# Feed-forward rows sorted by expert and gathered in tiles of 128, weights addressed by a register, output projection of two blocks moved up

## The chip, the cores and the metric

The kernel runs on one core of one Trainium2 chip. The metric is the device time of one execution in microseconds (us), the median of several runs. TensorE is called PE, VectorE DVE, ScalarE ACT, GpSimd POOL and SyncE SP, as in the profile. SP computes nothing here; it issues DMAs.

## The reference

One transformer layer on 2048 rows of 256 numbers (fp32). Attention has 16 heads of 128; its four weight matrices are stored as codes times scales for blocks of 32 input rows. The feed-forward part is a mixture of 8 experts with an inner size of 176. A router scores the experts, the two best are kept, and their outputs are summed with weights.

```python
def attn(x):   # q, k, v, out: w = codes * repeat(scales, 32)
    scores = einsum('bqhd,bkhd->bhqk', q, k) / sqrt(128)
    return mxfp4_matmul(softmax(scores) @ v, wo) + bo
def ffn(x):
    probs = softmax(x @ Wr)                    # 8 experts
    topk_w, topk_idx = top_k(probs, 2); topk_w /= topk_w.sum(-1)
    combine = sum over k of topk_w * one_hot(topk_idx, 8)
    h = silu(x @ Wg[e]) * (x @ Wu[e])          # every expert, 256 -> 176
    return sum over e of combine[:, e] * (h @ Wd[e])
x = x + layernorm(attn(layernorm(x)))
x = x + layernorm(ffn(layernorm(x)))
```

The reference computes all eight experts for every row; six of the eight have the weight zero in each row.

## The kernel before, in words

Everything is written out by hand in one program: a manual schedule, in which the order of the Python calls is the order of the instructions on each engine. The rows form 4 blocks (`b`) of 512, each of 4 tiles of 128.

The attention loop (`for g in range(NS + 2)`, 256 steps of one head and one tile of 128 query rows) takes some 1590 of the 1877 us. Each step makes scores in two halves (L453 to L457), a row maximum on DVE (L458), exponentials on ACT (L469), and a high and a low fp16 part of the probabilities (L483 on ACT, L498 on DVE), which two DMA transposes on SP's queue (L486, L502) turn into `pt`. The product with v (`pv_unit`, `pv_part`, L517 to L519) follows 13 half-steps behind (`PVLAG`). A finished head and block is cast on POOL (L531, L532) into `o`, a high and a low fp16 part, and stored by POOL's queue to `ot_d` in DRAM (L533). In the last head, `late(t)` also loads and dequantizes `wo`, loads the gate weights `wg` in four pieces (`load_gu`, L612) and splits each into a rounded part and a remainder in fp32r[...] (`split_gu`, `split_piece`: ACT L603, POOL L605), and begins to load block 0's `oi` (`load_oi`, L632), the attention output in pieces of four heads and 256 rows, on SP's queue.

After the last scores, `pv_unit(UEND)` to `pv_unit(UEND + 8)` finish the last block. Between them lie, for block 0, the output projection (`op_pass`, `op_mm`, L759: 64 products of 256 columns for half a block), the residual and both norms (`ln_a` to `ln_c`), the transposes of the normed rows (`tr`, L821) and the router (`router_a` to `router_d`). The router keeps the two best experts and writes a table of weights, 8 experts by 512 rows, to DRAM (`ct_d`, L886). The output projection of block 1 follows, then the loop.

The feed-forward loop (`for q in range(4 * NCH + 2)`) runs over 4 blocks and 11 chunks of 128 of the 8 x 176 = 1408 inner columns of all experts. `gate_up(b, c)` makes 12 products of 512 columns (L914: gate and up, two halves of the input, three products of high and low parts each), then a sigmoid (ACT L934), three multiplications on DVE (L935, L936, L939), one with `cu`, the routing weight spread over the chunk's rows by `load_cu` (L897), and a split into a rounded part (ACT L927) and a remainder (POOL L928). `down(b, c)`, two chunks later, adds 12 products of 256 columns (L953) to a block's sum. Output projection, norms and routers of blocks 2 and 3 are hooked into the chunks of earlier blocks (`FIRST`, `PREP`, `PREP2`); `fin1`, `fin2` (L786) and `fin_last` norm the sum and add it.

PE, ACT, DVE, POOL and SP each work through their own queue in order; a tile pool with few buffers makes a writer wait for the last reader. `psS` and `psA` are the pools of PSUM, where products are summed.

Of the kernel before, what the change touches and what calls it, by code (L numbers as in the profile page):

```python
# [33 lines left out]
POOL_COLS = 512  # L34
# [3 lines left out]
def sandwich(  # L38
# [28 lines left out]
    ct_d = [dram.tile([E, 512], F32, name=f"ct_d{b}") for b in range(4)]  # L67
# [9 lines left out]
    def rstd_of(mv, n, pool):  # L77
        v = pool.tile([128, n], F32, name="ln_v")
        nc.vector.tensor_scalar(v, mv[:, :, 1], EPS, None, ALU.add)
        r = pool.tile([128, n], F32, name="ln_r")  # L80
        nc.gpsimd.tensor_tensor(r, v, nhalf[:, :n], ALU.pow)
        return r
# [9 lines left out]
    rw = const.tile([128, 2, 2, E], F32R)  # L92
    res = const.tile([128, 2, NH], F32)

    def tail_consts(i):
# [5 lines left out]
        else:  # L101
# [6 lines left out]
            nc.gpsimd.tensor_tensor(rw[:, 1], rst, rw[:, 0].bitcast(F32), ALU.subtract)  # L108

# [48 lines left out]
    psS = ctx.enter_context(tc.tile_pool(name="psS", bufs=3, space=PSUM))  # L158
# [443 lines left out]
    def split_piece(dst, stg, on_pool):  # L602
        nc.scalar.copy(dst[0], stg)  # L603
        eng = nc.gpsimd if on_pool else nc.vector
        eng.tensor_tensor(dst[1], stg, dst[0].bitcast(F32), ALU.subtract)  # L605

    gu_raw = {}

    def load_gu(src, i, pool, tag, bufs, eng=None):
        kc, eh = divmod(i, 2)  # L610
        stg = pool.tile([128, 4, I], F32, name="gu_raw", tag=tag, bufs=bufs)
        (eng or nc.sync).dma_start(  # L612
            out=stg,
            in_=src.rearrange("e (kc p) i -> kc p e i", p=128)[kc][:, 4 * eh : 4 * eh + 4],
        )
        return stg

    def split_gu(dst, i, stg, on_pool):
        kc, eh = divmod(i, 2)
        cs = slice(4 * I * eh, 4 * I * eh + 4 * I)  # L620
        split_piece(
            (dst[:, 0, kc, cs], dst[:, 1, kc, cs]),
            stg.rearrange("p e i -> p (e i)"), on_pool,
        )

    OIN = {}

    def load_oi(b, half, j, tag="kT"):
        oi = kqv.tile(
            [128, 4, 2, 256], HP, name="oi", tag=tag, bufs={"kT": 8, "v": 7}[tag]  # L630
        )
        nc.sync.dma_start(  # L632
            out=oi, in_=ot_d[b][:, 4 * j : 4 * j + 4, :, bass.ts(half, 256)]
        )
        OIN[(b, half, j)] = oi

# [4 lines left out]
    gw = None  # L641
# [3 lines left out]
    WG_LOAD = (7, 9, 10, 11)  # L645

    def late(t):
        nonlocal gw
        if t in WO_LOAD:
            load_wo(3 + WO_LOAD.index(t), kqv, ("kT", "kT"), 8)  # L650
        if t - 1 in WO_LOAD:
            dequant_wo(3 + WO_LOAD.index(t - 1))
        if t == 13:
            bias_row2(gst.pop("b3"))
        if t == 12:
            gst["b3"] = bias_row()
        if t == 9:
            proj_ctx.close()
            rp = ctx.enter_context(tc.tile_pool(name="gw", bufs=1, side="right"))
            gw = rp.tile([128, 2, 2, EI], F32R)  # L660
        if 10 <= t < 14:
            split_gu(gw, t - 10, gst.pop(t - 10), True)
        if t in WG_LOAD:
            i = WG_LOAD.index(t)
            gst[i] = load_gu(wg, i, kqv, "kT", 8)
        if t == 9:
            load_oi(0, 1, 0, "v")
        if 11 <= t < 15:
            load_oi(0, 0, t - 11)

    X1 = {}
    XV = x.rearrange("b (c t p) d -> p (b c) t d", p=128, t=4)

    defer = False
    prev2 = None
    for g in range(NS + 2):
# [10 lines left out]
        if g == NS:  # L687
            load_oi(0, 1, 1)
            load_oi(0, 1, 2)
            load_oi(0, 1, 3)  # L690
# [41 lines left out]
        if g == NS:  # L732
            X1[0] = kqv.tile([128, 4, D], F32, name="x1_0", tag="kT", bufs=8)
            nc.sync.dma_start(out=X1[0], in_=XV[:, 0])
    UEND = 2 * (NS + 2)


    AT, MV, XT, CT = {}, {}, {}, {}

    OPS = {}  # L740

    def aux_psum(shape, dtype, name, tag):
        if tag == "s":
            return psS.tile(shape, dtype, name=name + "_s", tag="s", bufs=3)
        return psA.tile(shape, dtype, name=name, tag=tag)

    def op_mm(b, half, js, tag="pj"):
        if js[0] == 0:
            if half == 0:
                AT[b] = uwp.tile([128, 4, D], F32, name="at", bufs=2)  # L750
                MV[b] = small.tile([128, 4, 2], F32, name="mv")
            OPS[(b, half)] = aux_psum([128, 2, D], F32, "op", tag)
        ps = OPS[(b, half)]
        for j in js:
            oi = OIN.pop((b, half, j))
            for t in range(2):
                for hh in range(4):
                    for hl in range(2):
                        nc.tensor.matmul(  # L759
                            ps[:, t], oi[:, hh, hl, bass.ts(t, 128)],  # L760
                            wo[j // 2][:, 4 * (j % 2) + hh, :],
                            start=(j == 0 and t == 0 and hh == 0 and hl == 0),
                            stop=(j == 3 and t == 1 and hh == 3 and hl == 1),
                        )
        if js[-1] == 3:
            at = AT[b]
            tt = slice(2 * half, 2 * half + 2)
            nc.vector.scalar_tensor_tensor(
                at[:, tt], ps, sig[:, 0, 2:3],
                crow.unsqueeze(1).to_broadcast([128, 2, D]), ALU.mult, ALU.add,  # L770
            )
            stats(at, MV[b], 2 * half, 2 * half + 2)

    def op_pass(b, half, tag="pj"):
        op_mm(b, half, (0, 1, 2, 3), tag)

    def stats(src, mv, t0, t1):
        bs = small.tile([128, 4, 6], F32, name="bs")
        for t in range(t0, t1):
            nc.vector.bn_stats(bs[:, t], src[:, t, :])  # L780
        for t in range(t0, t1):
            nc.vector.bn_aggr(mv[:, t, :], bs[:, t])

    def norm(dst, src, mv, r):
        for t in range(4):
            nc.vector.tensor_scalar(  # L786
                dst[:, t, :], src[:, t, :], mv[:, t, 0:1], r[:, t : t + 1],
                ALU.subtract, ALU.mult,
            )

    R1, R2, MV2 = {}, {}, {}

    def ln_a(b):
        R1[b] = rstd_of(MV[b], 4, small)

    def ln_b1(b):
        norm(AT[b], AT[b], MV[b], R1[b])
        nc.vector.tensor_tensor(X1[b], AT[b], X1[b], ALU.add)

    def ln_b2(b):  # L800
        MV2[b] = small.tile([128, 4, 2], F32, name="mv2")
        stats(X1[b], MV2[b], 0, 4)
        R2[b] = rstd_of(MV2[b], 4, small)

    def ln_c(b):
        norm(AT[b], X1[b], MV2[b], R2[b])

    def tr(b, kc, tag="pj"):
        xn = AT[b]
        if kc == 0 and b == 0:  # L810
            XT[b] = [
                kqv.tile([128, 2, 512], F32R, name="xT0", tag="v", bufs=7)
                for _ in range(2)
            ]
        elif kc == 0:
            xt = tl.tile([128, 2, 2, 512], F32R, name="xT", bufs=2)
            XT[b] = [xt[:, 0], xt[:, 1]]
        xh, xl = XT[b]
        ps = aux_psum([128, 512], F32, "trp", tag)
        for t in range(4):  # L820
            nc.tensor.transpose(ps[:, bass.ts(t, 128)], xn[:, t, bass.ts(kc, 128)], ident)  # L821
        nc.scalar.copy(xh[:, kc], ps)
        nc.vector.tensor_tensor(xl[:, kc], ps, xh[:, kc].bitcast(F32), ALU.subtract)

    LGT, LG, CW = {}, {}, {}

    def router_a(b, tag="pj"):
        xT = XT[b]
        ps = aux_psum([8, 512], F32, "rp", tag)
        n = 0  # L830
        for kc in range(2):
            for a, w in ((0, 0), (1, 0), (0, 1)):
                nc.tensor.matmul(
                    ps, rw[:, w, kc, :], xT[a][:, kc, :], start=(n == 0), stop=(n == 5)
                )
                n += 1
        if b == 0:
            LGT[b] = kqv.tile([8, 512], F32, name="lgT0", tag="v", bufs=7)
        else:
            LGT[b] = tl.tile([8, 512], F32, name="lgT", tag="sg", bufs=3)  # L840
        nc.scalar.copy(LGT[b], ps)

    def router_b(b, tag="pj"):
        ps = aux_psum([128, 4, 8], F32, "lgp", tag)
        for t in range(4):
            nc.tensor.transpose(ps[:, t], LGT[b][:, bass.ts(t, 128)], ident[:8, :8])
        lg = small.tile([128, 4, 8], F32, name="lg", bufs=1)
        nc.vector.tensor_copy(lg, ps)
        mx = small.tile([128, 4, 8], F32, name="mx", bufs=1)
        ix = small.tile([128, 4, 8], U32, name="ix", bufs=1)  # L850
        for t in range(4):
            nc.vector.max(mx[:, t, :], lg[:, t, :])
# [166 lines left out]
    for j in range(4):  # L1019
        load_oi(1, 0, j)  # L1020
# [154 lines left out]
```

## Time and profile before

| | us |
|---|---|
| median of 3 runs | 1890.71 |
| lowest, highest | 1884.35, 1891.69 |
| profiled execution, its own time | 1879.05 |
| its span, first to last instruction | 1877.3 |
| last scores end at about | 1582 |
| first and last product of the feed-forward loop | 1640.7, 1870 |
| granted TensorE clock, mean | 0.99 |

The profile shows one execution. Each engine's busy time counts neither waiting nor sequencer work. Times in the stage table and the timelines count from the span's start. "Idle before, releaser" says how long an engine stood still ahead of an instruction, and what ended the wait. In the chain of waits each step is followed back to what released it.

### The profile page before, as it was taken

How to read it: one execution, taken by the hardware profiler on the slowest of the kernel's cores; microseconds unless marked ns; L12 is line 12 of the kernel's file. 1: busy time of each engine (PE TensorE's matmuls, PEld its weight loads, DVE VectorE, ACT ScalarE, POOL GpSimd, SP SyncE). 2: the span in 40 equal slices, each digit the busy share in tenths (PEclk: the TensorE clock that was granted, in tenths of full speed). 3: DMA queues.
4: the chain of work that ended last, by engine and by line, in shares of the span. 5: the costliest groups of instructions: out<-in, count | busy, mean ns of one | idle time of the engine just before them, and what ended most of it. 6: DMA issues, size and time to landing. Idle time of an engine off the chain costs nothing. (4 is left out here: it accounts for less than half of the span.)

```text
span 1877.3 us, 25533 instructions
## 1 busy us (share of the span) xinstructions
PE 1794.1 (96%) x8890; PEld 936.0 (50%) x8890; DVE 1632.4 (87%) x2267; ACT 1365.5 (73%) x1730; POOL 907.5 (48%) x893
## 2 busy tenths in 40 slices
PE   7899999999999999999999999999999988899998
PEld 4344444444444444444444444444444434588887
DVE  7999989998999899998999999889999886458566
ACT  5888878888888788887888888778888776123232
POOL 3554574457544654465445644564444342233222
PEclk9999999999999999999999999999999999999999
DMA  3999999999999999999999999999999999982121
GB/s 91 190 193 190 189 202 198 190 189 202 196 191 189 193 195 191 192 201 193 188 190 205 197 189 192 183 202 194 191 186 205 208 220 219 259 236 69 55 71 57
DMA packets 1133345, 342.31 MB, mean 182 GB/s; under 512 B 1070896, under 2 KB 1120768, under 8 KB 1133216
## 3 DMA queue, kind: packets, MB, share of 16 engines
q1 hardware_dynamic: 1120528, 310.53, 90.4%
q0 software_dynamic: 9584, 27.82, 5.9%
q10 hardware_dynamic: 3104, 2.33, 0.5%
q8 instruction: 70, 1.15, 0.2%
q14 instruction: 59, 0.48, 0.1%
HBM read 53.22 MB, written 18.94 MB: 38 GB/s over the span
## 5 line engine op out<-in xcount | busy, mean ns | idle before, releaser
L498 DVE SCALAR_TENSOR_TENSOR pl<-p,m,ph 128x1024 f16<-128x1024 f32 x512 | 731.6, 1429 | 50.2 <-DMA pt<-pl 43.9
L469 ACT ACTIVATE p<-s,m,ssc 128x1024 f32<-128x1024 f32 x512 | 611.9, 1199 | 192.6 <-DVE m L462 158.9
L458 DVE TENSOR_REDUCE m<-s 128x1 f32<-128x1024 f32 x512 | 622.0, 1215 | 23.2 <-PE s L457 22.7
L483 ACT ACTIVATE ph<-p,m 128x2048 f16<-128x2048 f32 x256 | 513.0, 2004 | 84.7 <-issue 30.2
L518 PE MATMUL pv<-pt,v 128*128 128x512 f16 x1024 | 391.2, 382 | 27.9 <-DMA pt<-pl 27.9
L453 PE MATMUL s<-kT,qT 128*128 128x512 f16 x1024 | 389.9, 381 | 16.9 <-ACT p L469 13.9
L517 PE MATMUL pv<-pt,v 128*128 128x512 f16 x1024 | 390.6, 381 | 7.4 <-DMA pt<-ph 5.3
L519 PE MATMUL pv<-pt,v 128*128 128x512 f16 x1024 | 391.2, 382 | 0.0
L454 PE MATMUL s<-kT,qT 128*128 128x512 f16 x1024 | 389.8, 381 | 0.0
L457 PE MATMUL s<-kT,qT 128*128 128x512 f16 x1024 | 305.3, 380 | 0.0
L205 POOL CAST qT<-t 128x512 f16<-128x512 f32 x63 | 86.4, 1371 | 247.2 <-ACT t L204 247.2
L236 POOL CAST v<-t 128x256 f16<-128x256 f32 (+1 forms) x105 | 54.3, 517 | 271.8 <-ACT t L235 271.8
L518 PEld LDWEIGHTS <-v 128*128 128x128 f16 x1024 | 100.7, 98 | 153.8 <-issue 29.4
L454 PEld LDWEIGHTS <-qT 128*128 128x128 f16 x1024 | 100.4, 98 | 135.2 <-issue 33.4
L517 PEld LDWEIGHTS <-v 128*128 128x128 f16 x1024 | 100.6, 98 | 130.8 <-issue 7.0
L519 PEld LDWEIGHTS <-v 128*128 128x128 f16 x1024 | 100.7, 98 | 123.6 <-issue 7.6
L457 PEld LDWEIGHTS <-qT 128*128 128x128 f16 x1024 | 100.5, 98 | 121.8 <-issue 1.7
L453 PEld LDWEIGHTS <-qT 128*128 128x128 f16 x1024 | 100.6, 98 | 111.3 <-issue 3.2
L237 POOL TENSOR_TENSOR v<-t,v 128x256 f16<-128x256 f32 (+1 forms) x105 | 146.8, 1398 | 8.4
L928 POOL TENSOR_TENSOR hh<-sg,hh 128x512 fp32r<-128x512 f32 x42 | 54.5, 1298 | 144.6 <-ACT hh L927 99.4
L927 ACT CAST hh<-sg 128x512 fp32r<-128x512 f32 (+1 forms) x45 | 27.5, 611 | 118.4 <-DVE sg L939 118.4
L206 POOL TENSOR_TENSOR kT<-t,kT 128x512 f16<-128x512 f32 x60 | 107.8, 1796 | 5.0
(184 smaller groups left out, 2019.4 us busy)
## 6 DMA issues: line engine op xcount, KB each, us to landing
oi<-ot_d SPq DMA_DIRECT2D x32, 512.0 KB, 6.9
ot_d<-o POOLq DMA_DIRECT2D x63, 256.0 KB, 4.1
pt<-ph SPq DMA_TRANSPOSE x256, 5.1
pt<-pl SPq DMA_TRANSPOSE x256, 4.7
cu<-ct_d SPq DMA_DIRECT2D x16, 256.0 KB, 3.9
xt<-in_L_attn_x SPq DMA_DIRECT2D x4, 512.0 KB, 5.6
wos<-in_L_attn_wo_scales ACTq DMA_DIRECT2D x32, 64.0 KB, 4.5
woc<-in_L_attn_wo_codes SPq DMA_DIRECT2D x8, 256.0 KB, 3.5
```

What stands on the lines that cost most here:

```text
L206: nc.gpsimd.tensor_tensor(t[:, 1, :], t32, t[:, 0, :], ALU.subtract)
L237: nc.gpsimd.tensor_tensor(v[:, 1, sl, :], t32, v[:, 0, sl, :], ALU.subtract)
L453: nc.tensor.matmul(s[:, j, :], q[:, 0, qc], k[:, 0, :], start=True, stop=False)
L454: nc.tensor.matmul(s[:, j, :], q[:, 0, qc], k[:, 1, :], start=False, stop=False)
L457: nc.tensor.matmul(s[:, j, :], q[:, 1, qc], k[:, 0, :], start=False, stop=True)
L458: nc.vector.tensor_reduce(m[:, half : half + 1], s, AX.XY, ALU.max)
L469: nc.scalar.activation(p[:, bass.ts(i, 1024)], s, AF.Exp, bias=m[:, 2:3], scale=ssc[:, 0:1], accum_out=m[:, 3 + i : 4 + i],)
L483: nc.scalar.activation(ph, p, AF.Copy, scale=m[:, 6:7])
L498: nc.vector.scalar_tensor_tensor(pl[:, cs], p[:, cs], m[:, 6:7], ph[:, cs], ALU.mult, ALU.subtract)
L517: nc.tensor.matmul(ps, vh, d[:, :, c, :], start=(c == 0), stop=False)
L518: nc.tensor.matmul(ps, vh, d[:, :, 16 + c, :], start=False, stop=False)
L519: nc.tensor.matmul(ps, vl, d[:, :, c, :], start=False, stop=(c == 15))
```

## The change

The feed-forward part is rebuilt for the chosen experts alone.

- **Sorting.** Two groups of 1024 rows (two blocks) are sorted apart. `router_c` makes one-hot rows of the two chosen experts. `places(G)` counts, by products with a triangle and with ones, how many rows of each expert lie ahead of a row, rounds each expert's count up to a multiple of 128, and so gives each of the 2048 row-expert pairs a place (`POS`) among 23 tiles of 128. `slot_rows(G)` inverts this: which row lies in which place (`ROWS`). `TE[G]` holds for each tile the expert's offset in the weights. 23 tiles hold any routing.
- **Rows.** `rows16(b)` writes each normed row (times 64) as a high and a low fp16 part to DRAM (`xr_d`). `load_xg(q)` gathers 128 rows by an indirect DMA on POOL's queue, `turn_xg(q)` turns them by a DMA transpose on SP's queue.
- **Tiles.** 46 tiles in place of 44 chunks. `ff_up(q)` loads the tile's offset from SBUF into a register of PE and makes 6 products of 352 columns (gate and up of one expert side by side), addressed by the register; then a sigmoid on ACT and two DVE operations. `ff_tr(q - 1)` turns the result by two fp32 transposes, and `ff_down(q - 2)` makes 6 products of 256 columns, addressed too; the sum is copied by ACT and stored by SP to `ys_d`. In the program each of the 552 addressed products has an instruction of register arithmetic ahead of it on PE.
- **Result.** `gather(b, u)` fetches both results of a row by indirect DMAs on POOL (four per 256 rows), `combine` weights, sums and takes statistics, `finish_rows` norms, adds and stores. The routing weight is applied here.
- **Weights** become fp16 high and low parts instead of fp32r ones, scaled by powers of two that are found at run time (`largest`, `scale_gu_a` to `_c`, `squares`, `scale_d_a`, `_b`); they are loaded and split after the attention (`load_raw`, `split_raw`).
- **Moves.** The output projection of blocks 2 and 3 goes from the loop to the stage ahead of it; that of block 1 goes ahead of `pv_unit(UEND + 1)`. Block 0's eight `oi` loads go from SP's queue to POOL's. Two of four norms go from DVE to ACT (`normed`). `load_cu`, `ct_d`, `fin*` and the splits of the last head are gone.

The diff, cut to its core:

```diff
     def load_oi(b, half, j, tag="kT", eng=None):
...
-        nc.sync.dma_start(
+        (eng or nc.gpsimd).dma_start(
             out=oi, in_=ot_d[b][:, 4 * j : 4 * j + 4, :, bass.ts(half, 256)]
...
     def late(t):
...
-        if 10 <= t < 14:
-            split_gu(gw, t - 10, gst.pop(t - 10), True)
-        if t in WG_LOAD:
-            i = WG_LOAD.index(t)
-            gst[i] = load_gu(wg, i, kqv, "kT", 8)
-        if t == 9:
-            load_oi(0, 1, 0, "v")
-        if 11 <= t < 15:
-            load_oi(0, 0, t - 11)
+        if t == 11:
+            loads(0, 0, (0, 1, 2), "g")
+        if t == 13:
+            loads(0, 0, (3,), "g")
+            loads(0, 1)
...
+    def slot_rows(G, tag="pj"):
+        lo, hi = SL.pop(G)
+        ps = aux_psum([128, GT], F32, "slp", tag)
+        for i in range(16):
+            nc.tensor.matmul(ps, lo[:, i], hi[:, i], start=(i == 0), stop=(i == 15))
+        ROWS[G] = P["ff"].tile([128, GT], I32, name="rows", bufs=2)
+        nc.vector.tensor_copy(ROWS[G], ps)
...
+    def load_xg(q):
+        G, j = divmod(q, GT)
+        xr = P["ff"].tile([128, 512], HP, name="xq", bufs=5)
+        nc.gpsimd.indirect_dma_start(
+            out=xr, out_offset=None, in_=xr_d[G],
+            in_offset=bass.IndirectOffsetOnAxis(ap=ROWS[G][:, j : j + 1], axis=0),
+        )
+        XQ[q] = xr
+
+    def turn_xg(q):
+        XG[q] = P["ff"].tile([128, 4, 128], HP, name="xg", bufs=4)
+        nc.sync.dma_start_transpose(out=XG[q], in_=XQ.pop(q))
+
+    def ff_up(q):
+        G, j = divmod(q, GT)
+        REG[q] = nc.values_load(
+            TE[G][0:1, j : j + 1], engines=(mybir.EngineType.PE,), min_val=0,
...
+        ps = P["psF"].tile([128, 2 * I], F32, name="gup", bufs=2)
+        n = 0
+        for kc in range(2):
+            for a, w in ((0, 0), (0, 1), (1, 0)):
+                nc.tensor.matmul(
+                    ps, xg[:, 2 * a + kc, :], GU[(w, kc)].rearrange("p e n -> p (e n)")[
+                        :, bass.ds(REG[q], 2 * I)
+                    ],
+                    start=(n == 0), stop=(n == 5),
+                )
+                n += 1
+        sg = P["ff"].tile([128, I], F32, name="sg", bufs=2)
+        nc.scalar.activation(sg, ps[:, :I], AF.Sigmoid, scale=sgs)
+        h = P["ff"].tile([128, I], F32, name="h", bufs=2)
+        nc.vector.tensor_tensor(sg, sg, ps[:, :I], ALU.mult)
+        nc.vector.scalar_tensor_tensor(h, sg, HC, ps[:, I : 2 * I], ALU.mult, ALU.mult)
...
+    def ff_tr(q):
...
+        for c in range(2):
+            nc.tensor.transpose(ps[:, c], h[:, bass.ts(c, IC)], ident)
+        hh = P["ff"].tile([IC, 2, 2, 128], HP, name="hh", bufs=2)
+        nc.scalar.copy(hh[:, 0], ps)
+        nc.vector.tensor_tensor(hh[:, 1], ps, hh[:, 0], ALU.subtract)
...
+    def ff_down(q):
...
+                nc.tensor.matmul(
+                    ps, hh[:, a, c, :], dwv[:IC, w, c, bass.ds(REG[q], D)],
+                    start=(n == 0), stop=(n == 5),
+                )
...
+        nc.scalar.copy(y, ps)
+        nc.sync.dma_start(out=ys_d[G][bass.ts(j, 128)], in_=y)
...
+    def gather(b, u):
...
+            for k in range(2):
+                nc.gpsimd.indirect_dma_start(
+                    out=yg[:, i, k, :], out_offset=None, in_=ys_d[G],
...
     pv_unit(UEND)
+    op_mm(0, 0, ALL, "pj")
+    loads(1, 0, ALL, "g", nc.sync)
+    op_mm(0, 1, ALL, "s")
+    loads(1, 1, ALL, "kT", nc.sync)
...
+    op_mm(1, 0, ALL, "s")
+    ln_b(0)
+    op_mm(1, 1, ALL, "s")
...
+    op_mm(2, 1, (1, 2), "s")
+    slot_rows(0)
+    for q in range(5):
+        load_xg(q)
...
+    op_mm(3, 0, ALL, "s")
+    for q in range(4):
+        turn_xg(q)
...
+    op_mm(3, 1, ALL, "s")
...
+    NQ = 2 * GT
+    for q in range(NQ + 2):
+        if q < NQ:
+            ff_up(q)
+        if 1 <= q < NQ + 1:
+            ff_tr(q - 1)
+        if q >= 2:
+            ff_down(q - 2)
+        for f in HOOK.get(q, []):
+            f()
+        if q + 5 < NQ:
+            load_xg(q + 5)
+        if q + 4 < NQ:
+            turn_xg(q + 4)
+    for i in range(4):
+        gather(2 + i // 2, i % 2)
+    for i in range(4):
+        combine(2 + i // 2, i % 2)
...
```

`HOOK` hangs transposes, routers and norms of blocks 2 and 3 on tiles 1 to 13, the second sort on tiles 14 and 16, and gathers and combines of the first group on tiles 27 to 43.

## The prediction

> **What bounds the kernel now.** I read the page first, then the stage table, then the chain of waits in the tail, then the timelines of PE, SP and POOL around the end of the attention.
>
> ```profile
> span 1877.3 us, 25533 instructions
> PE 1794.1 (96%) x8890; PEld 936.0 (50%) x8890; DVE 1632.4 (87%) x2267; ACT 1365.5 (73%) x1730; POOL 907.5 (48%) x893
> ```
>
> TensorE is busy 96% of the span, but the change touches only what follows the last scores, so the limit must be read there.
>
> ```profile
> core 0: us, PE busy (x) PEld busy (x) DVE busy (x) ACT busy (x) POOL busy (x), PEclk, DMA share, GB/s
> 1589.50:1640.70 51.20, 43.74 (x328) 31.74 (x326) 20.72 (x59) 10.16 (x15) 13.98 (x11) 0.93 1.03 254
> 1640.70:1724.00 83.30, 80.05 (x491) 68.71 (x489) 54.60 (x119) 22.27 (x39) 26.95 (x20) 0.98 0.60 164
> 1724.00:1870.00 146.00, 145.58 (x892) 126.65 (x890) 95.14 (x211) 40.82 (x72) 41.30 (x33) 1.00 0.21 64
> 1870.00:1877.30 7.30, 0.03 (x1) 0.00 (x0) 3.66 (x12) 1.02 (x2) 1.39 (x2) 0.82 0.21 72
> ```
>
> The first row is the stage between attention and feed-forward: the DMA share is 1.03, the engines are not full. The next two are the feed-forward loop: PE is full, DVE at 65% and DMA at 21% in its second part. The last is the closing norm.
>
> ```profile
> 1820.66 2.75 PE gup L914 x12
> 1823.40 1.43 PE dps L953 x12
> 1824.84 2.75 PE gup L914 x12
> 1827.58 1.43 PE dps L953 x12
> ```
>
> In the chain nothing but matmuls follows matmuls: one chunk costs 2.75 + 1.43 = 4.18 us. 44 chunks are 184 us; the output projection of blocks 2 and 3, 4 x 7.0 us, lies in the loop too.
>
> ```profile
> 1593.54 3.50 SPq L632 DMA_DIRECT2D oi<-ot_d  x3
> ...
> 1605.99 3.66 SPq L502 DMA_TRANSPOSE pt<-pl  x1
> ...
> 1610.91 6.70 SPq L632 DMA_DIRECT2D oi<-ot_d  x4
> ...
> 1593.41 0.56 POOL L533 DMA_DIRECT2D ot_d<-o  x1 [0.30 <-POOL o L532]
> ```
>
> The columns are start, duration and what was issued. The last low-part transposes of the attention stand behind three loads. Four attention-output loads of 512 KB hold SP's queue for 6.70 us, 1.68 us each or 312 GB/s: that is the rate of this stage. A plain store costs POOL 0.56 us.
>
> [...] after 5.46 us idle at 1564.87 the score products stand 0.43 us apart, later 0.216. [...] the 512 products of L759 run at 109 ns per pair of weight load and product. [...] here a 256 KB store lands after 4.1 us (median).
>
> **The change, part by part.**
>
> *Last head.* Four loads of `wg` (352 KB) and four splits (0.77 us ACT, 1.98 us POOL each) leave it, and eight `oi` loads go from SP to POOL. Three of those loads stood for 3.5 us ahead of the last low-part transposes on SP (1593.54), so these end at about 1606.3 instead of 1609.7: −3 us. On POOL the third load of the eight waits for a store to land (4.1 us); behind it stand the casts of o for two later blocks, awaited only by loads after 1606: nothing, up to +4 if that cover is gone. The new constants are nine POOL and one DVE instruction of about 1 us in head 0, where POOL is half idle: nothing, at most +2.
>
> *Stage before the loop.* Now all eight output-projection passes lie here: PE 8 x 7.0 = 56, eight pv units 6 x 0.216 each = 10.4, transposes and routers 5: 71 us from 1589.5, plus waits for block 1's loads, which are queued behind the transposes (first usable at about 1612, PE idle some 8 us in place of the old 7). That alone would end near 1670. SP has more: 24 `oi` loads x 1.68 = 40 us; twelve weight loads, 4.3 MB at 312 GB/s = 14; four x blocks 7; two stores of rows 3; from 1606.3 this is 1670. SP then meets one real wait: the store of block 1's rows needs DVE (about 3 us late) and everything of blocks 2 and 3 stands behind it. Four gather-transposes at the end of the queue cost 4 and land 3 later: **the loop starts at about 1680**. Sorting (some 20 small DVE operations near 0.2 us plus the 128x2048 comparison, about 2.2 us by the 1.05 ns per column of the DVE rows), slot matmuls, five gathers and the weight splits (ACT 8 x 0.77 + 4 x 1.0, DVE 8 x 0.9 + 4 x 1.2) lie beside it; DVE sums to about 60 us of 85. Without that cover the sort chain, 15 us from router to first gathered tile, would show: range 1672 to 1695.
>
> *Loop.* 44 chunks (184 us) and 28 us of projections go; 46 tiles come, 23 for each half of the rows. On the array one tile is 6 products of 352 columns and 6 of 256, at L759's 109 ns per 256: 6 x 0.150 + 6 x 0.109 = 1.55, and two fp32 transposes 0.22: 1.77 us. ACT: 0.4 + 2 x 0.38 (the 128x256 forms) = 1.15. DVE: 2 x 0.33 + 0.42 = 1.08. SP: a transpose a quarter of the old size, 0.5 to 0.8, and a store 0.4. POOL: one gather. All are below the array. But each product takes its address from a register: one fused register instruction ahead of each of the twelve, and a load of the register from SBUF once a tile, in order on PE's sequencer, and behind it all of PE's queue. The trace has no such instruction. [...] Low: hidden, 1.77. High: [...] 3.8. I take [...] **2.64 us a tile**: 46 x 2.64 = 121. Hooks on PE (transposes, routers of blocks 2 and 3, 5 us) fit into the array's slack; the second sort and four combines are 4 to 9 us DVE bursts against less than 2 us of pipeline depth: +6. Loop 127, end at 1807.
>
> *End.* In place of 7.3 us: y copied and stored, 3; then sixteen gathers that all wait for the last store. A gather's POOL time is not in the trace: low 0.56 (plain store)[...], taken 1.2: 19 us. Landing 3, and the last combine, power, norm, sum and store 3.1 + 1.2 + 1.0 + 0.7 + 2.2 plus handovers: 10. Together 35 (25 to 48).
>
> *Sum.* 1680 + 127 + 35 = 1842 against 1877.3: −35 us. The profiled execution took 1879.05, 0.6% below the median 1890.71 of the three runs; −35 from the median is 1856.
>
> **The rivals.**
> - *Register work hidden, array sets the pace.* [...] Against: 12 products leave 148 ns each for product, weight load and register instruction. 46 x 1.77 + hooks 5 + bursts 6 = 93; end 1680 + 93 + 35 = 1808: −69, **1822**.
> - *Slower: the register path costs more than the products it saves.* With the high prices 46 x 3.8 + 6 = 181; 1680 + 181 + 35 = 1896: +19, **1910**. It decides from (1877.3 − 1680 − 35 − 6) / 46 = 3.40 us a tile on. [...] Against: it takes the worst of each price.
> - *POOL becomes the bound.* 41 x-gathers and 16 y-gathers in the loop, 16 behind it. At 2.0 us the loop's 114 still fits beside 127 and the tail gains 13: −22, **1868**; from 2.2 us on POOL sets the loop. For: POOL is idle only half the time now. Against: its plain issues are 0.55 to 0.73.
> - *The change doesn't do what it says:* excluded in the amount of work, as 46 tiles of 128 rows run whatever the routing (5888 rows against 16384 row-expert pairs).
>
> **How the numbers follow.** About 9.5 us, 0.5%, is what a measurement can tell from none. Forecast, 2.2 to 3.2 us a tile: 0.45, its own range 1835 to 1882. Array-paced: 0.25. Slower: 0.18. POOL: 0.12. Faster: 0.41 + 0.25 + 0.07 = 0.73; same: 0.04 + 0.04 = 0.08; slower 0.18 and a rest of 0.01 from POOL: 0.19. The range reaches from just below the array-paced case to the slower case without its last end: 1812 to 1908.
>
> **What would show it.** Right: the loop begins near 1680 with PE waiting for `oi` or the gather-transpose; in it PE is busy below 80%, its idle time given to "issue" or PE's sequencer rather than to DVE, ACT or a DMA, and a tile takes 2.2 to 3.2 us; sixteen gathers close the chain. Array-paced: tile 1.8, PE above 90%. Slower: tile above 3.4 with the same kind of idle time. POOL: PE waits for the transposed rows, these for gathers of 2 us. I am wrong if the loop starts after 1700, if a tile is paced by a DMA's landing, or if the attention itself moves by more than 5 us.

## The result, and the profile after

| us | before | after |
|---|---|---|
| median of the same four rounds | 1887.78 | 1909.06 |
| lowest, highest | 1884.35, 1891.69 | 1903.6, 1917.91 |
| profiled execution, its span | 1877.3 | 1910.4 |

The ratio is 1.0117 (95% interval 1.0068 to 1.0165): slower, where the forecast was faster. In later rounds, beside some of the experiments, the changed kernel (`e8_again`) took 1892.68 against 1883.59 us: ratio 1.0042 (1.0011 to 1.0073, 13 runs). How much slower it is differs; that it is slower does not. The experiments ran on three chips beside runs of the kernel before: `e1_sp`, `e1b_spread`, `e2_fixed` and `e3_tail` on one, `e8_again`, `e4_store`, `e5_bursts` and `e6_merge` on a second, the others on a third, so the changed kernel itself stands beside those of the second alone. The ratios leave out runs in a slower state, of which there were three (1902.75 to 1905.53 us, all of `e10_before_pool`).

> The changed kernel unaltered, for a second trace and more runs beside the same runs of the kernel before as the three that follow. If the hold-up in the last head belongs to the kernel: a transpose of 15 to 28 us on SP's queue behind POOL's loads again, and a ratio of 1.007 to 1.016. If it was an accident of one execution: no transpose over 8 us there, and a ratio near 1.000.

Its hold-up is a transpose of 18.75 us behind another of 6.37, and the ratio lies below the range expected.

The first lines of the page of the changed kernel, and its table by stage. The rows are: from `bias_row` in the last head to the first projection product, the stage before the loop, the loop, the tail.

```profile
span 1910.4 us, 25817 instructions
PE 1716.9 (90%) x8517; PEld 843.9 (44%) x8517; DVE 1614.2 (84%) x2353; ACT 1390.1 (73%) x1830; POOL 916.3 (48%) x937
```

```profile
core 0: us, PE busy (x) PEld busy (x) DVE busy (x) ACT busy (x) POOL busy (x), PEclk, DMA share, GB/s
1565.10:1616.80 51.70, 26.74 (x122) 11.93 (x122) 21.53 (x30) 19.60 (x23) 5.05 (x6) 0.77 1.13 185
1616.80:1715.30 98.50, 79.88 (x627) 60.44 (x626) 60.29 (x176) 33.40 (x54) 17.06 (x16) 0.94 0.94 239
1715.30:1868.50 153.20, 113.85 (x705) 75.45 (x704) 79.10 (x263) 62.72 (x167) 60.82 (x63) 0.85 0.59 137
1868.50:1910.40 41.90, 0.22 (x2) 0.00 (x0) 14.16 (x44) 4.73 (x9) 18.01 (x20) 0.53 0.27 82
```

TensorE has 77 us less work over the span and the span is 33 us longer. The work that was to go has gone: what is new is standing still. In the first row PE is busy for 26.74 of 51.70 us, in the loop for 113.85 of 153.20, at a mean clock of 0.85.

Executions differ by more than 20 us ahead of the last head alone. So they are compared below by the time from one mark to the next. "Head" runs from the issue of the last load of projection codes (`woc`) to the first projection product; the others are the rows above. This issue comes between 1536.7 and 1560.2 us in the twelve traces of the changed kernel and its variants, at 1539.5 and 1540.5 us in the two of the kernel before; what the new constants in head 0 add to it, no run isolates.

| us | woc issued at | head | stage | loop | tail |
|---|---|---|---|---|---|
| before | 1539.5 | 50.0 | 287.8 for the three | | |
| forecast | | 50 | 90.5 | 127 | 35 |
| after | 1547.7 | 69.1 | 98.5 | 153.2 | 41.9 |
| after, second trace | 1560.2 | 62.0 | 97.8 | 140.0 | 42.4 |

(The forecast left the first projection product at 1589.5 us; its −3 us belong to the transposes in the stage.) Against before, the first trace is +8.2 by where it stood at the mark, +19.1 in the head and +5.8 in the rest (98.5 + 153.2 + 41.9 = 293.6 against 287.8): 33.1. The second has +12.0 in the head, and the rest is 7.6 us shorter than before.

**The head.** Timeline of SP's queue in the changed kernel, then of POOL's (start, duration, what was issued):

```profile
1553.93 2.24 SPq L537 DMA_TRANSPOSE pt<-pl  x1
1556.27 4.61 SPq L521 DMA_TRANSPOSE pt<-ph  x1
1560.97 27.23 SPq L537 DMA_TRANSPOSE pt<-pl  x1
1588.29 5.12 SPq L521 DMA_TRANSPOSE pt<-ph  x1
```

```profile
1556.48 2.67 POOL L646 DMA_DIRECT2D oig<-ot_d  x3
1562.51 0.88 POOL L646 DMA_DIRECT2D oig<-ot_d  x1 [3.35 <-DMA ot_d<-o]
1563.38 3.50 POOL L646 DMA_DIRECT2D oi<-ot_d  x4
```

POOL issues eight 512 KB loads in 10 us, and from there one transpose takes 27.23 us. In the kernel before, with its loads on SP's queue, the transposes of this head take 1.7 to 5.5 us:

```profile
1564.30 0.49 SPq L632 DMA_DIRECT2D oi<-ot_d  x1
1564.88 4.19 SPq L502 DMA_TRANSPOSE pt<-pl  x1
```

In the changed kernel the buffers of the softmax come free only behind the long transpose, and DVE stands 27.15 us, ACT and PE behind it:

```profile
1593.73 1.28 DVE L533 SCALAR_TENSOR_TENSOR pl<-p,m,ph 128x1024 f16<-128x1024 f32 x1 [27.15 <-DMA pt<-pl]
```

**The loop.** Groups of PE in the loop: line, operation, count, busy time and mean, then the idle time before them and what ended it.

```profile
L1070 PE MATMUL gup<-gu,xg 128*128 x276 | 58.4, 356 | 22.0 <-DMA xg<-xq 12.7 <-DVE at L720 5.5 <-PE yps L1102 2.1
L1102 PE MATMUL yps<-dw_t,hh 88*128 x276 | 44.7, 301 | 1.0 <-ACT hh L1090 0.6 <-issue 0.2
L1088 PE MATMUL hT<-ident,h 128*88 128x128 f32 x92 | 20.5, 309 | 21.1 <-DVE h L1081 21.1
```

44 us of idle time, of which 5.5 (DVE at L720) stand ahead of the loop's first product and so belong to the stage. Almost nothing is given to "issue", where the forecast put the register work. It is given to DVE (21.1 us) and to the transposed rows (12.7 us). Four of the waits, from PE's timeline:

```profile
1773.25 0.63 PE L1088 MATMUL hT<-ident,h 128*88 128x128 f32 x2 [4.57 <-DVE h L1081]
1808.46 0.39 PE L1088 MATMUL hT<-ident,h 128*88 128x128 f32 x2 [3.40 <-DVE h L1081]
1830.74 1.92 PE L1070 MATMUL gup<-gu,xg 128*128 x6 [3.88 <-DMA xg<-xq]
1855.59 1.06 PE L1070 MATMUL gup<-gu,xg 128*128 x6 [2.26 <-DMA xg<-xq]
```

The first stands behind `places(1)`, a row of small DVE operations and, in its `slots`, one on 2048 columns (2.28 us). The second is put down to DVE, but DVE stood idle too, for a sigmoid of ACT, and ACT stood for something that the profile doesn't name ("remote" is another core or an unknown queue):

```profile
1806.89 0.37 ACT L1108 COPY yo<-yps 128x256 f32<-128x256 f32 x1 [4.57 <-remote]
1839.96 0.41 ACT L1078 ACTIVATE sg<-gup,sgs 128x176 f32<-128x176 f32 x1 [3.92 <-remote]
```

ACT has 13.1 us of such waits in this loop, all in its second half, and none in the loop of the second trace, which is 13.2 us shorter. The four traces of the chip of `e1_sp` have 8.1 to 12.5 us of them and loops of 150.9 to 162.3 us; the traces of the two other chips have none. So this part of the loop doesn't belong to the program alone; what ACT waits for stays open.

The third wait shows a second price: after 3.88 us of standing still the six products take 1.92 us, after 2.26 us they take 1.06; the granted clock over the 5 us from their start is 0.50 and 1.00. In PE's timelines of ten loops (all but those of `e9_all_fixed` and `e11_nomerge`) there are 29 waits of 3.44 us or more behind the loop's first product, and what followed was slower each time: six products (once five) took 1.47 to 1.94 us instead of 1.05, two transposes 0.57 to 0.66 instead of 0.38. For shorter waits the length does not decide. In `e5_bursts`:

```profile
1800.25 1.05 PE L1111 MATMUL gup<-gu,xg 128*128 x6 [3.40 <-DMA xg<-xq]
1822.31 1.91 PE L1111 MATMUL gup<-gu,xg 128*128 x6 [2.41 <-DMA xg<-xq]
```

### The profile page after: what moved, and what is told of

Read it like the earlier page. It is cut to its first block, busy times and chain, and to the rows that moved or that the text cites. A ratio compares the mean times of both kernels' runs of the same rounds, so it can differ in the third digit from the quotient of the medians.

```text
span 1910.4 us, 25817 instructions
## 1 busy us (share of the span) xinstructions
PE 1716.9 (90%) x8517; PEld 843.9 (44%) x8517; DVE 1614.2 (84%) x2353; ACT 1390.1 (73%) x1830; POOL 916.3 (48%) x937
## 5 line engine op out<-in xcount | busy, mean ns | idle before, releaser
L272 POOL TENSOR_TENSOR v<-t,v 128x256 f16<-128x256 f32 (+1 forms) x105 | 151.2, 1440 | 8.4
L504 ACT ACTIVATION_READ_ACCUMULATOR p<-s,m,ssc 128x1 f32 x512 | 99.1, 194 | 0.0
L240 POOL CAST kT<-t 128x512 f16<-128x512 f32 x60 | 44.4, 739 | 98.1 <-ACT t L239 98.0
```

Of the source, the lines that this page charges most:

```text
L240: nc.gpsimd.tensor_copy(t[:, 0, :], t32)
L272: nc.gpsimd.tensor_tensor(v[:, 1, sl, :], t32, v[:, 0, sl, :], ALU.subtract)
L504: nc.scalar.activation(p[:, bass.ts(i, 1024)], s, AF.Exp, bias=m[:, 2:3], scale=ssc[:, 0:1], accum_out=m[:, 3 + i : 4 + i],)
```

## The experiments

**1. The eight loads from SP again (`e1_sp`).**

```
-loads(0, 0, (0, 1, 2), "g")            # t == 11
+loads(0, 0, (0, 1, 2), "g", nc.sync)
-loads(0, 0, (3,), "g"); loads(0, 1)    # t == 13
+loads(0, 0, (3,), "g", nc.sync); loads(0, 1, ALL, "kT", nc.sync)
```

> The eight loads of rows for the output projection in the last head (three at step 11, five at step 13) are issued from SP's queue instead of POOL's, at the same places; all else is the changed kernel. If the queue is the cause of the 27 us hold-up (loads of POOL's software queue keep SP's transposes from their share of the DMA engines): the long transpose of 27.23 us falls to at most 8 us, the last head is 19 to 27 us shorter, and the time is 1882 to 1890 us. If the volume is the cause (4 MB more through the DMA engines in three steps, whatever queue they are in): the transposes behind them still wait about 8 x 1.7 = 14 us or more, and the time is 1897 us or above.

1894.64 against 1884.20 us: 1.0063 (1.0041 to 1.0085). SP's timeline, at the place of the long transpose:

```profile
1572.43 6.95 SPq L646 DMA_DIRECT2D oi<-ot_d  x4
1579.47 4.72 SPq L537 DMA_TRANSPOSE pt<-pl  x1
1584.28 1.84 SPq L521 DMA_TRANSPOSE pt<-ph  x1
```

Four of the same eight loads hold SP for 6.95 us, and the transpose behind them takes 4.72 us. The head falls to 44.9 us: the volume alone is not the cause. The time is above what this theory had (1882 to 1890). The stage grew from 98.5 to 107.6 us, so about 9 us of the saving were given back there (the same stage of `e5_bursts`, 105.1 us, has a DMA share of 0.99). The profiled executions of the seven kernels here with these loads on SP have heads of 44.2 to 49.1 us, the four with all eight on POOL 61.9 to 69.1.

**2. Fewer at a time on POOL (`e1b_spread`).**

```
+if 11 <= t < 15: loads(0, 0, (t - 11,), "g")      # POOL, one a step
+loads(0, 1, ALL, "kT", nc.sync)                   # after the last scores
```

> Of the eight loads in the last head, four stay on POOL's queue, but one a step at steps 11 to 14 instead of three and five at once; the other four are issued from SP after the last transpose. If it is the software queue as such that starves the transposes, each load holds up a transpose by some 3 us and 8 to 14 us of the 27 stay: 1894 to 1898 us. If it is the pile of eight at once, nearly all goes, and the four at the end cost up to 6 us before the second half of block 0: 1882 to 1889 us.

1900.88 us: 1.0085 (1.0059 to 1.0110), above what either theory had; head 56.0 us. POOL's and SP's timelines:

```profile
1553.95 2.67 POOL L646 DMA_DIRECT2D oig<-ot_d  x3
```

```profile
1558.50 16.36 SPq L537 DMA_TRANSPOSE pt<-pl  x1
```

The edit did not do what it was to do: three of the four loads went out together. Nothing on POOL ties a step of the program to a time; behind the cast of `o` and its store it issued three steps' loads in one go. It still tells something: three loads at once cost a transpose of 16.36 us, so the pile need not be eight. After the fourth load, which went out alone at 1590.80 us, the longest took 6.41 us.

**3. The same queue in the kernel before (`e10_before_pool`).**

```
-load_oi(0, 1, 0, "v")                    # t == 9
+load_oi(0, 1, 0, "v", nc.gpsimd)
-load_oi(0, 0, t - 11)                    # 11 <= t < 15
+load_oi(0, 0, t - 11, eng=nc.gpsimd)
```

> The kernel before, with its five loads of projection rows in the last head (one at step 9, four at steps 11 to 14) issued from POOL's queue instead of SP's; nothing else is changed. If loads of that queue starve SP's transposes of the DMA engines: a transpose of over 12 us in the last head and 6 to 16 us more, 1890 to 1900 us. If what held up the changed kernel was only that it moved eight loads into three steps: within 3 us of the kernel before.

1889.51 against 1882.20 us: 1.0031 (1.0004 to 1.0058). POOL's timeline:

```profile
1557.04 0.93 POOL L632 DMA_DIRECT2D oi<-ot_d  x1
1568.37 0.91 POOL L632 DMA_DIRECT2D oi<-ot_d  x1
1575.89 0.90 POOL L632 DMA_DIRECT2D oi<-ot_d  x1
```

Here POOL has other work in every step, so the loads really are apart. No transpose in this head is over 5.70 us, and the head is 51.4 us against 50.0. The forecast of a transpose over 12 us fell: loads of POOL's queue that come singly do little to the transposes. So it takes both, the queue of POOL and several loads in it at once. The time fits neither theory well: 0.31% are some 6 us, where one had 6 to 16 and the other at most 3, and the head of this trace grew by 1.4 alone. What the two look like in the DMA engines between 1560 and 1588 us (packets, MB, then the time that a queue's packets took, as a share of 16 engines), first the changed kernel, then this one:

```profile
DMA packets 3307, 3.83 MB, mean 137 GB/s; under 512 B 2522, under 2 KB 2522, under 8 KB 3306
q0 software_dynamic: 872, 3.21, 65.3%
q1 hardware_dynamic: 2434, 0.62, 47.8%
```

```profile
DMA packets 15372, 6.44 MB, mean 230 GB/s; under 512 B 14040, under 2 KB 14794, under 8 KB 15369
q0 software_dynamic: 655, 2.36, 30.5%
q1 hardware_dynamic: 14714, 4.05, 86.4%
```

q0 is POOL's queue, q1 that of SP. With the pile, SP's queue gets 0.62 MB through in 28 us instead of 4.05. Its packets are 0.25 KB, POOL's 3.7 KB. In these 28 us the transposes got the smaller part of the bytes (0.62 against 3.21 MB), though the larger part of the packets (2434 against 872); how the engines divide their time between two queues was not shown. The packets of both queues are slower too: POOL's take 335 ns each here (0.653 x 16 x 28 us / 872) against 209 ns in the second kernel, SP's 88 (0.478 x 16 x 28 us / 2434) against 26. Why, stays open.

**4. Constants instead of registers (`e2_fixed`, and `e9_all_fixed` on the improved version of experiment 9).**

```
-REG[q] = nc.values_load(TE[G][0:1, j : j + 1], engines=(PE,), ...)
+REG[q] = (8 * j // GT) * 2 * I
```

> The expert of each tile is a constant of the program instead of a register loaded on the PE's queue (the weights of a fixed expert are used for each tile, so rows meet the wrong expert; every product and every size stays). If the loop is paced by register work as the forecast had it (2.64 us a tile against 1.77 of the array): 46 x 0.87 = 40 us less, 1869 us. If the register work is hidden behind the array and the waits for DVE and for transposes: within 3 us of the changed kernel, 1906 to 1912 us.

1897.04 us: 1.0065 (1.0045 to 1.0084), loop 150.9 us. In time that lies between the two theories, and as the changed kernel itself measured 1.0117 and 1.0042 it decides nothing. The trace does: the loop is 2.3 us shorter than in the first trace, not 40, and idle times of the same size are left (5.68 us at `places(1)`, 4.29, 4.11 and 4.42 later).

> The version before this one with the expert of each tile a constant of the program instead of a register loaded on PE's queue (rows meet the weights of a wrong expert; every product and size stays). If register work is hidden even when the other stalls are gone: loop within 3 us of that version's, time within 4 us. If it is the next limit of a tile (0.2 to 0.4 us each, 46 tiles): loop 9 to 18 us shorter.

1864.25 us, 0.9914 (0.9881 to 0.9946), against 0.9900 (0.9869 to 0.9930) for the version with registers: no gain in time. Loop 127.5 against 129.3 us. But where no wait lies between tiles, the register is visible. PE's timeline of the improved version, with registers, then with constants:

```profile
1752.54 1.05 PE L1111 MATMUL gup<-gu,xg 128*128 x6
1753.43 0.38 PE L1129 MATMUL hT<-ident,h 128*88 128x128 f32 x2
1753.65 0.82 PE L1143 MATMUL yps<-dw_t,hh 88*128 x6
1754.52 1.06 PE L1111 MATMUL gup<-gu,xg 128*128 x6
```

```profile
1764.74 1.06 PE L1107 MATMUL gup<-gu,xg 128*128 128x352 f16 x6
1765.64 0.38 PE L1125 MATMUL hT<-ident,h 128*88 128x128 f32 x2
1765.86 0.82 PE L1139 MATMUL yps<-dw_t,hh 88*128 88x256 f16 x6
1766.52 1.06 PE L1107 MATMUL gup<-gu,xg 128*128 128x352 f16 x6
```

From one tile to the next it is 1.98 us with registers and 1.78 us with constants. So the visible register work is 0.20 us in such a tile, ahead of the next tile's first product, and not 0.87. It can be hidden wholly: of the tiles of `e8_again` with no wait and at full clock, ten take 1.91 to 2.05 us and three 1.78 to 1.81, all with registers. Over 46 tiles 0.20 us would be 9 us, of which the loop is 1.8 shorter: in the kernel with constants the waits for transposed rows grew from 10.4 to 16.2 us.

**5. The store that stood in SP's queue (`e4_store`, on `e1_sp`).**

```
-rows16(1)                     # copy, subtract, store
+rows16(1, send=False)
 loads(2, 1, ALL, "v", nc.sync)
 load_raw(2)
+send16(1)
```

> On top of the loads from SP: the store of block 1's 16-bit rows, which stood 13.4 us at the head of SP's queue until DVE had its rows ready, is issued after the four loads of block 2's second half and the four of the down weights, instead of ahead of them. If that wait sets the end of the stage (the loads of block 3 come last there, and PE waits for them three times): the stage before the loop falls from 107.6 us to 98 to 101 us, and the time from 1894.6 us by 5 to 9. If the stage ends by POOL's first gathers or DVE's splitting of weights instead: within 2 us of it.

1882.23 against 1883.59 us: 0.9998 (0.9979 to 1.0017); the changed kernel in the same rounds is the second trace above, 1.0042. So the loads from SP (with this edit) are worth some 10 us there. But the stage is 104.4 us, no shorter than in two kernels of the same rounds without the edit (105.1 and 104.2): the store in the queue, which stood 13.37 us in `e1_sp`, cost nothing. A likely reason is in the row of this stage in its table, a DMA share of 0.95:

```profile
1597.60:1702.00 104.40, 81.21 (x627) 61.91 (x626) 64.97 (x180) 35.33 (x55) 16.52 (x16) 0.92 0.95 239
```

The stage moves 25 MB at 239 GB/s, and the DMA engines are left little room that a different order could use. The 239 GB/s were measured; the forecast took 312.

**6. Smaller pieces in the first half of the loop (`e5_bursts`, on `e1_sp`).** `ln_b`, `ln_c` and `rows16` of block 3 and `slots` of blocks 2 and 3 are cut into parts, about one part a tile.

```
-2: [ln_b(3)], 6: [ln_c(3), rows16(3)], 14: [places(1)], 16: [slot_rows(1)]
+2: [ln_b3(3, 0)], 3: [ln_b3(3, 1)], 4: [ln_b3(3, 2)], 5: [ln_b3(3, 3)],
+6: [ln_c2(3, 0)], 8: [ln_c2(3, 1)], 10: [rows16p(3, 0)], ...
+14: [places(1)], 15: [slots(1)], 16: [slots_lo(1)], 18: [slot_rows(1)]
```

> On top of the loads from SP: the work of blocks 2 and 3 inside the first half of the loop (norms, 16-bit rows, places, slots) is cut into pieces of one DVE or ACT operation of 0.4 to 2.3 us each and hung on different tiles; nothing is left out. If bursts on DVE are what stops the pipeline in the first half (gaps of 2.71, 3.65, 2.60 and 4.92 us before transposes of h, 13.9 us): the loop falls from 152.9 us to 141 to 145 us. If a piece costs its tile the same delay as before, because DVE has no slack: over 150 us.

1875.49 against 1883.59 us: 0.9966 (0.9947 to 0.9985). Loop 131.3 us, where two kernels of the same rounds with the old hooks have 140.0 and 142.3: 9 to 11 us shorter, as the bursts theory had it (the 152.9 us it started from belong to another chip, and have ACT's unnamed waits in them). The gain lies where the edit is: up to the first product of tile 23 it takes 64.4 us against 72.3 and 71.9, after it 66.9 against 67.7 and 70.4. The mean clock in the loop is 0.95 instead of 0.87 to 0.89.

**7. Gathers one a tile in the second half (`e6_merge`, on `e1_sp`).**

```
-GT+4+4i: gather(b, u)   GT+7+4i: combine   GT+8+4i: finish_rows with its store
+GT+3+4i+n: gather1(b, u, n), n = 0..3   GT+9+4i: combine
+GT+11+4i: finish_rows   GT+12+4i: out_rows
```

> On top of the loads from SP: in the second half of the loop the sixteen gathers of group 0's results go out one a tile instead of four at once, each unit is combined three tiles after its last gather instead of three tiles after all four were queued, and its store is issued one tile after its rows are done. If the second half loses its time to DVE standing behind gathers and to transposes standing behind those stores (gaps of 3.38, 1.44, 4.39, 1.75 and 3.44 us, 14.4 us): the loop falls from 152.9 us to 138 to 145 us. If POOL is the bound there (two gathers a tile, 2.5 us): 150 us or more.

1881.96 us: 1.0001 (0.9977 to 1.0026). Loop 138.8 us against 140.0 and 142.3: most of the expected gain is missing. At least one of the gaps that were to go, 3.38 us in `e1_sp`, stood behind an unnamed wait of ACT (4.88 us), which this chip doesn't have. POOL's timeline in the second half:

```profile
1786.87 0.94 POOL L1132 DMA_INDIRECT yg<-ys_d,pos  x1 [0.30 <-issue]
1788.12 0.95 POOL L1049 DMA_INDIRECT xq<-xr_d,rows  x1 [0.30 <-issue]
1791.92 0.72 POOL L86 TENSOR_TENSOR ln_r<-ln_v,nhalf 128x2 f32<-128x2 f32 x1 [2.85 <-DVE ln_v L84]
1792.83 1.01 POOL L1132 DMA_INDIRECT yg<-ys_d,pos  x1 [0.19 <-issue]
1794.14 0.97 POOL L1049 DMA_INDIRECT xq<-xr_d,rows  x1 [0.30 <-issue]
```

A gather every 1.25 us, two for a tile of 2.0, and a power (L86, the root in the norm) that stands 2.85 us at DVE with the next gathers behind it: while both kinds of gather run, here from 1774 to 1819 us, POOL sets the pace, 2.5 us a tile.

**8. Order of the tail (`e3_tail`, on the changed kernel).**

```
-gather x4;  combine, finish x4
+gather, gather, combine, gather, finish, combine, gather, finish, combine, ...
```

> Only the order after the loop is changed: gathers of two units, then combining of the first, gather of the third, and so on, so that the power operations of POOL stand between the gathers and not behind all sixteen. If the tail is held by the powers that wait behind the gathers: the last unit is combined within 8 us of its gather and the end comes 5 to 8 us earlier, 1901 to 1904 us. If the sixteen gathers alone set the end: within 2 us of the changed kernel.

1906.96 us: 1.0103 (1.0008 to 1.0198, four runs), too wide to tell the theories apart. The tail is 40.3 us against 41.9. In the changed kernel the powers do stand behind the gathers, by POOL's timeline:

```profile
1890.09 0.95 POOL L1119 DMA_INDIRECT yg<-ys_d,pos  x1 [0.30 <-issue]
1891.34 0.95 POOL L1119 DMA_INDIRECT yg<-ys_d,pos  x1 [0.30 <-issue]
1892.31 1.41 POOL L86 TENSOR_TENSOR ln_r<-ln_v,nhalf 128x2 f32<-128x2 f32 x2
```

Moved between them, they lengthen the row of gathers from 19.8 to 22.1 us, and what follows the last gather falls from 18.1 to 13.5 us. So in the traces the queueing was worth 1.6 us and not 5 to 8: most of what it cost moved into the row of gathers.

**9. An improved version (`e7_all`), and the same without experiment 7 (`e11_nomerge`).** Experiments 1, 6, 7 and 8 together; in experiment 7 the power is hung one tile later than its variance; block 2's 16-bit rows are made in pieces in the loop instead of ahead of it; half of the down weights are split after the last projection rows instead of ahead of them.

> A version of the changed kernel with what the runs so far support: the eight loads from SP; the work of blocks 2 and 3 cut into pieces; gathers of group 0's results one a tile with combining two units of work later, the power of each unit hung one tile behind its variance so that POOL doesn't stand at it; the first half of the down weights split before the last output rows and the second half after; gathers and powers interleaved at the end. If the parts add (10 us of bursts, 3 of merging, 2 at the end of the stage, 1.5 in the tail, on the ratio 1.000 of the loads from SP): 1865 to 1872 us, loop 122 to 130 us. If POOL is the bound of the second half (36 gathers of 1.25 us in 20 tiles): loop not under 130 us, and 1872 to 1878 us.

> The improved version without its change to the gathers of the second half: four at once, combining as in the changed kernel. If spreading them pays: its loop is 3 to 8 us longer than the improved version's, 1869 to 1879 us. If POOL's number of gathers is the bound in that half, however they are placed: within 2 us of the improved version.

1861.73 against 1882.20 us: 0.9900 (0.9869 to 0.9930), and without the spread gathers 1869.53: 0.9933 (0.9913 to 0.9953). Both beat the kernel before, the first by more than was expected (1865 to 1872 us). Loops 129.3 and 133.1 us, tails 38.0 and 38.0. Spreading the gathers looks worth 4 us in the traces, but the intervals overlap.

| us | woc issued at | head | stage | loop | tail |
|---|---|---|---|---|---|
| `e7_all` | 1544.6 | 48.7 | 102.2 | 129.3 | 38.0 |

Against before its rest is 269.5 instead of 287.8 us and its head 1.3 us shorter, 19.6 us together; the medians are 20.5 us apart. So much is this version of the change worth, with the loads back on SP and DVE's work in small pieces.

## Why the prediction was wrong

The sum was 1842 us of span; measured were 1910.4 and 1902.4. From the `woc` mark on, the forecast had 302.5 us, the two traces 362.7 and 342.2. The misses, first and second trace: head 19.1 and 12.0 us, stage 8.0 and 7.3, loop 26.2 and 13.0, tail 6.9 and 7.4. No one term used up the forecast gain of 35 us. With the loads back on SP the ratio is 1.0063 on one chip and 0.9998 and 1.0001 on another (with one edit more each), not faster.

- **Last head, "−3": wrong.** The loads were costed by what they leave (SP's queue, 3 us) and by POOL's own time ("nothing, up to +4"). What was put at nothing is what they do to the transposes on the other queue: one of 19 to 27 us with all eight on POOL, +12 to +19 us in the head. Nor did SP need to lose them: with the loads kept on SP, in the new places, the heads are 1 to 6 us shorter than before, though the stage behind takes 104 to 108 us there instead of 98. The forecast's own line that it is wrong "if the attention itself moves by more than 5 us" names this.
- **Stage, "about 1680", 90.5 us: 98.** The bound was named rightly, DMA and SP's queue. The rate of 312 GB/s was taken from four loads in a row; the stage's mean is 239. The wait for block 1's rows, costed at 3 us, held SP for 15.17 us in the first trace; in the version of experiment 5 such a wait cost nothing.
- **Loop, 127 us: 153 and 140.** Two terms were off, in opposite directions. The register term, 2.64 us a tile, was the author's estimate, which no trace had shown, and it was too high: a tile takes 1.98 at most places where PE doesn't wait. The array's 1.77 was right (1.78 with constants). The addition for bursts, +6, was too low. 46 x 1.98 is 91 us, so 49 to 62 us are bursts, waits, the routers' small products and a lower clock (a mean of 0.85 and 0.89 in the two loops); cutting the bursts took away 9 to 11, and some 13 of the 62 go with ACT's unnamed waits. That the clock falls where PE stands still had no term. The sign that the forecast set for itself, idle time given to "issue", was not there.
- **Tail, 35 us: 42.** The gather at 1.2 us was right (0.95 busy, 1.25 from one to the next; 19.8 us for sixteen against 19). The 13 us after them were 18.1, with the powers queued behind the gathers on POOL; with the powers between them (experiment 8) 13.5 us follow, after a longer row of gathers.
- **The rivals.** "Slower" came true by its total, 1910 us against a median of 1909.06, by chance: it had a loop of 181 us from 1680 on, by 3.8 us a tile, an estimate that no trace had shown; measured were 153 from 1715 and 140 from 1720, and register work is the smallest of the terms. "Array sets the pace" was right about registers for nine tenths and wrong about everything else in the loop. "POOL becomes the bound" came true in part, in the second half of the loop (experiment 7), at 1.25 us a gather, not from the 2.2 us at which the forecast let it begin, and not at its 2.0, which no trace had shown: it counted the gathers over the whole loop, 57 in 127 us, and not where they fall, some 30 in the last 20 tiles.

What stays open is the rate in the pile of experiment 3, and what ACT waits for in the loops of 151 to 162 us.

## What to carry to other kernels

A transfer that is moved to another queue can hold up what the first queue still carries (here, with eight loads moved, one transpose took 27.23 us, where those of the kernel before take 1.7 to 5.5): ask what else is under way in the same microseconds, not only what the queue itself gains. When a loop is made shorter, side work that used to fit into it as one block may have to be cut to the new length of a step (worth 9 to 11 us in experiment 6); count it, and the work of every queue, by the half of the loop in which it falls. The steps of a program need not spread work over time: POOL issued the loads of three steps within 2.67 us in experiment 2, and singly, 3.7 to 11.3 us apart, where it had other work in between (experiment 3).

## What the runs showed of the hardware

- Three to eight 512 KB loads pending at once in POOL's queue stretch a 2 to 5 us transpose of SP's queue to 16 to 27 us, with the total rate down to 137 GB/s (first trace, 1560 to 1588 us; 230 in `e10_before_pool`). With the same loads in SP's queue (`e1_sp`) no transpose of that head took over 5.24 us, with five loads singly in POOL's queue, in the kernel before, none over 5.70.
- Where PE doesn't wait, a tile with twelve products addressed by a register takes mostly 1.98 us, with constant addresses 1.78; some tiles with registers take 1.78 too.
- A gather of 128 rows is 0.95 us of POOL and 1.25 us from one to the next, for rows of 1 KB from either source.
- After each of 29 waits of PE of 3.44 us or more, in ten loops, the products were slower: six (once five) took 1.47 to 1.94 us instead of 1.05, two transposes 0.57 to 0.66 instead of 0.38. Below that it went both ways: six products took 1.91 us after 2.41, 1.05 after 3.40.
